# Context attention: the last three head pairs regrouped one group of scores sooner, and the product banks weighed first in the gated part

## The chip, the cores and the metric

One core of a Trainium2 chip runs the whole program. The metric is device time in microseconds, the median of several executions; lower is better. TensorE (PE) multiplies, with its weight loads listed apart as PEld. VectorE (DVE), ScalarE (ACT) and GpSimd (POOL) do the elementwise work. SyncE (SP) computes nothing here: it issues DMA transfers, one after the other.

## The reference

A transformer block over x of shape (2, 1024, 256) with a context of shape (2, 154, 192), in float32, 16 heads of 64:

```python
h = layernorm(x, ln1);  x = attention(h, h,       sa_*) + x
h = layernorm(x, ln2);  x = attention(h, context, ca_*) + x
h = layernorm(x, ln3)
p = h @ ff_w1 + ff_b1
a, gate = p[..., :1024], p[..., 1024:]
out = (a * gelu(gate)) @ ff_w2 + ff_b2 + x
```

Attention is softmax(q kᵀ / 8) v for each head, and then a product with `wo`.

## The kernel before

The program is one long order written out by hand: no scheduler moves anything, and every engine runs its own instructions in the order in which the loops emit them. Self-attention fills the first two thirds of the span, then comes context attention, then the gated part (the feed-forward layer).

**Context attention** works on 16 units, one for each batch and pair of heads (8 pairs for each of 2 batches); below, "pair 13" is unit 13. The scores of a unit are made in three groups of token tiles (3, 3 and 2 tiles of 128), so there are 48 groups, counted by `c`; `CA` is 48 and `len(CG)` is 3. The loop over `c` emits, for each group, the scores (`sc`, L828), then maxima, exponentials and the scaling with the reciprocal sums. Two groups later `cross_drain` transposes the probabilities on VectorE into a ring of three units (`pT_ca`, L872).

**Regrouping.** `cross_regroup(c)` copies one unit's transposed probabilities from the ring into the buffer `pairs`, by eight DMAs of 128 KB issued from SyncE (L889). The buffer has two halves, `a2` = 0 and 1; the first four DMAs fill half 0, the last four half 1. There is one such buffer (a part of the tile `wf`), so a unit's regrouping must wait for the products of the unit before, which read it.

**Products.** `cross_weigh(c)` runs `cross_values` for two parts, `a2` = 0 and then 1. Part `a2` multiplies the values `v_ca` with half `a2` of `pairs` for two of the four quarters of the tokens, into two PSUM banks (`poc`, L908; quarters 0 and 2 in part 0, 1 and 3 in part 1). Part 0 takes its banks from the pool of sums (`sum_tile`, two banks), part 1 from the pool of products (`mm_tile`, two banks). The four banks are then copied into `o_ca` (L922): all on VectorE in context attention, in the gated part half on VectorE and half on ScalarE. One `o_ca` tile holds two pairs (`HP` is 2), and `out_piece` multiplies it with `ca_wo` into `py_ca` (L471), one product for each pair in turn; VectorE adds the result to x (L478).

A unit's last group is `c = 3 ui + 2`, transposed at `3 ui + 4`; its regrouping stands at `3 ui + 5`, its products at `3 ui + 7`. For the last units the count runs on into the gated part, where `c = 48 + k`: unit 14 is weighed at k = 1 and unit 15 at k = 5. `context_values`, once for every two units, makes a new `v_ca`; the six DMAs that complete it (L800, L805) are put on the list `later` and issued at the end of the same step, after `cross_regroup` in that step.

**The gated part** takes two steps for each block of 128 features. `gate_first` makes `pa`, `pb` and `pc` (L1029), where `pa` is in a product bank; `gate_second` adds to them, and ScalarE takes GELU from `pa` (L1066). Then, in each step:

```python
cross_drain(c)
if k % 2:
    cross_weigh(c - 1 if k == len(CG) + 2 else c)
cross_regroup(c)
```

`gate_first` of the next block asks for a product bank again, and so does each `py_ca` of the gated part. The dictionary `pools` is empty before the gated part and holds one entry from its beginning on.

Of the kernel before, what the change touches and what calls it, by code (L numbers as in the profile page):

```python
# [18 lines left out]
def tile_transformer_block(ctx: ExitStack, tc: tile.TileContext, a: dict, out: bass.AP):  # L19
# [11 lines left out]
    HP = NPAIR // NQ  # L31
# [182 lines left out]
    hT, vs, qk, oT = {}, {}, {}, {}  # L214
# [347 lines left out]
    def run(piece):  # L562
        done = piece()
        if done is not None:
            (adds if getattr(done, "adds", False) else stores).append(done)

    def flush(queue):
        for fn in queue:
            fn()
        queue.clear()  # L570
# [160 lines left out]
    CG = [(t, min(TG, NT - t)) for t in range(0, NT, TG)]  # L731
    CA = len(CG) * NU
# [144 lines left out]

    def cross_regroup(c):

        ui, n = divmod(c - len(CG) - 2, len(CG))  # L880
        if n != 0 or not 0 <= ui < NU:
            return
        for a2 in range(2):
            for a4 in range(P // KB):
                half, e = divmod(a4, 2)
                own = slice(a4 * KB, (a4 + 1) * KB)
                src = slice((2 * half + a2) * KB, (2 * half + a2 + 1) * KB)
                blocks = pTc["ring"][src, ui % 3, :2 * NM].rearrange("p (m e) j q -> p m e (j q)", e=2)
                nc.sync.dma_start(  # L889
                    out=pTc["pairs"][own, a2].rearrange("p m j q -> p m (j q)"), in_=blocks[:, :, e])  # L890

    def cross_values(ui, a2):

        b, pr = units[ui]
        v, v0 = vs["ca", b, pr // 2], pr % 2 * P
        if a2 == 0 and pr % HP == 0:
            oT["ca", b, pr // HP] = pt_.tile([P, HP, S], F32, tag="oT", name=f"o_ca{b}_{pr}")  # L900
        quarters = (a2, 2 + a2)
        po = {a4: (mm_tile if a2 else sum_tile)(f"poc_{ui}_{a4}") for a4 in quarters}
        for m in range(NM + 1):
            for a4 in quarters:
                r0 = a4 // 2 * QG
                r = slice(r0, r0 + QG)
                for j in range(2):
                    nc.tensor.matmul(  # L908
                        po[a4][j * DH:(j + 1) * DH, :NT * KB],
                        lhsT=v[r, m + a2 * (m == NM), v0 + j * DH:v0 + (j + 1) * DH],  # L910
                        rhs=pTc["pairs"][r, a2, m, j] if m < NM else
                        pTc["ring"][r, ui % 3, NB - 1, j, :],
                        start=(m == 0), stop=(m == NM),
                        tile_position=(r0, j * DH),
                    )
        dst = oT["ca", b, pr // HP][:, pr % HP, :].rearrange(
            "p (t a q) -> p t a q", a=P // KB, q=KB)

        def store():
            for a4 in quarters:  # L920
                copy = nc.scalar.copy if pools and a4 // 2 else nc.vector.tensor_copy
                copy(dst[:, :, a4, :], po[a4][:, :NT * KB].rearrange("p (t q) -> p t q", q=KB))  # L922

        return store
# [18 lines left out]
    def cross_weigh(c):  # L943

        ui, n = divmod(c - 2 * len(CG) - 1, len(CG))
        if n == 0 and 0 <= ui < NU:
            for part in range(2):
                run(lambda: cross_values(ui, part))
            flush(stores)

# [4 lines left out]
    wsum, wh, ub, psum, pools = {}, {}, {}, {}, {}  # L955
# [156 lines left out]
    with tc.manual_schedule():  # L1112
# [59 lines left out]
        for p in range(SA):  # L1172
# [19 lines left out]
            ui, n = divmod(p, 2 * SH)  # L1192
# [8 lines left out]
            if hg == LAG:  # L1201
# [5 lines left out]
                if n == SH + LAG and ui in (0, 1, NU - 1):  # L1207

                    pr = {0: 2, 1: 4, NU - 1: 6}[ui]
# [3 lines left out]
        for c in range(CA):  # L1213
# [13 lines left out]
            ui, n = divmod(c, len(CG))  # L1227
# [33 lines left out]
            elif c == 4:  # L1261
                run(lambda: self_values(2 * NU - 1, 1))
            elif n == 0 and ui:
                if nxt:
                    run(lambda: cross_queries(*nxt))
                else:
                    run_work(2, 0)
                run_work(0, 1)
            elif n == 1:

                spare["turned"] = True
                run_work(0, 1, sum_tile if outs else None)
                flush(stores)
                run_work(0, 0, n_sum=1)
                if ui % 2 == 0:
                    run(lambda: context_values(*units[ui]))
                run_work(1, 0)
                flush(adds)
                flush(stores)
                cross_weigh(c)  # L1280
            elif n == 2:
                run_work(0, 1, sum_tile if ui == HP + 1 else None)
                if c == SH + 1:
                    run_work(2, 0)
                elif ui == HP:
                    wo["ca"] = const.tile([P, NPAIR, D], F32, tag="wo", name="ca_wo")
                    later[:0] = [lambda i=i: nc.sync.dma_start(
                        out=wo["ca"][:, i, :], in_=w["ca_wo"][i * P:(i + 1) * P, :])
                        for i in range(NPAIR)]
            cross_regroup(c)  # L1290
            for _ in range(min(2, len(later))):
                later.pop(0)()
# [16 lines left out]
        for k in range(2 * FU):  # L1309
            c = CA + k  # L1310
            if k == 0:
                run_work(0, 0, n_sum=2)
            flush(adds)
            (gate_second if k % 2 else gate_first)(k // 2)
            flush(stores)
            flush(lates)
            if k == 2 * len(CG) + 1:
                norm_beside("ff", B - 1)
# [4 lines that stand above are left out]
            if k == len(CG) + 2:  # L1323
                out_pieces("ca", B - 1, NQ - 1, out_order("ca"))
            if k % (2 * NF) == NF and k < 2 * FU - 2 * NF:
                token_sums(k // (2 * NF) + 1)
            for _ in range(min(2, len(sums))):
                run(sum_slot)
            flush(stores)
            run_work(0 if k == 1 else 1 + k % 2, k % 2)  # L1330
            if later and (k <= len(CG) + 2 or k > 2 * NF):
                later.pop(0)()
# [37 lines left out]
```

## Time and profile before

| | |
|---|---|
| median of 3 runs | 1082.71 us (1082.28 to 1084.15) |
| the profiled execution | 1084.96 us, of which the span is 1083.2 us |
| granted TensorE clock | 1.000 over the span |
| 885 to 930 us: busy | PE 43.26, PEld 34.21, DVE 29.79, ACT 19.37, POOL 24.89 us; DMA share 0.36 |
| 930 to 1083 us: busy | PE 149.08, DVE 75.09, ACT 42.72, POOL 68.79 us; DMA share 0.04 |

Times in the profile are microseconds from the span's start. A line of the timeline gives the start, the length, the engine, the line of the kernel, the operation, the tiles (out<-in) and the number of instructions; in brackets stands how long the engine was idle just before, and what released it. SPq is SyncE's queue, and the length of one of its lines is that of issuing, not of the transfer. A releaser is inferred from semaphores: of a wait for several it names the one that came last by the profile. The busy time of TensorE is partly modelled, so a stall shows best in the gaps between weight loads. One float32 product shows as two weight loads and two matmuls.

### The profile page before, as it was taken

The numbers are of one execution on the slowest core, as the hardware profiler recorded it, in microseconds if no ns is written. First come the engines' busy times: TensorE is split into PE (matmuls) and PEld (weight loads), VectorE is DVE, ScalarE is ACT, GpSimd is POOL, SyncE is SP. The second block draws the span as 40 slices with busy tenths as digits, with TensorE's granted clock in tenths as the row PEclk, the third lists the DMA queues.
The fourth block names the chain that finished last, engine by engine and source line by source line (L and its number), as shares of the span: only waits on it lengthen the run. The fifth ranks groups of instructions, "written<-read, shape, count | busy, mean of one in ns | idle before, by whom it ended". The sixth has DMA issues, their size and how long they took to land.

```text
span 1083.2 us, 46388 instructions
## 1 busy us (share of the span) xinstructions
PE 1067.0 (99%) x19156; PEld 703.2 (65%) x19156; DVE 878.7 (81%) x1297; ACT 643.5 (59%) x2062; POOL 727.1 (67%) x1552
## 2 busy tenths in 40 slices
PE   8999999999999999999999999999999999999998
PEld 6556556556565565575665655566776677788887
DVE  5799999998989989999999889968877887654442
ACT  5766666777667657666776776656555554242321
POOL 2677777777777777677777777776756785475321
PEclk9999999999999999999999999999999999999999
DMA  3222122112111121111111101136765545000000
GB/s 91 68 70 52 39 48 53 43 43 50 32 43 34 30 50 38 34 43 34 33 42 25 43 14 38 29 79 150 191 157 125 119 107 118 1 10 15 11 14 30
DMA packets 104724, 60.81 MB, mean 56 GB/s; under 512 B 32378, under 2 KB 95298, under 8 KB 104514
## 3 DMA queue, kind: packets, MB, share of 16 engines
q1 hardware_dynamic: 103138, 57.07, 22.2%
q8 instruction: 151, 2.47, 1.0%
q10 hardware_dynamic: 1376, 0.79, 0.2%
q14 instruction: 59, 0.48, 0.1%
HBM read 27.91 MB, written 2.10 MB: 28 GB/s over the span
## 4 chain that ended last, share of the span: by engine, by line
PE 83%; DVE 4%; POOL 4%; DMA 3%; SPq 2%; ACT 2%; issue 1%; POOLq 0%; DVEq 0%; ACTq 0%
PE po L549 18%; PE s L497 17%; PE py_sa L471 5%; PE pf L1095 5%; PE py_ca L471 5%; PE pk_sa L366 4%; PE pv_sa L397 4%; PE poc L908 4%; PE pq_ca L366 4%; PE pq_sa L366 4%; PE pb L1029 4%; DMA st<-st 3%; PE sc L828 2%; PE pa L1029 2%; PE pc L1029 2%; SPq L518 2%
## 5 line engine op out<-in xcount | busy, mean ns | idle before, releaser
L619 POOL TENSOR_SCALAR p<-p,rd,ee 128x512 f32<-128x512 f32 x512 | 390.4, 768 | 90.8 <-DVE rd L609 87.7
L508 ACT ACTIVATE p<-s,st 128x512 f32<-128x512 f32 x512 | 345.0, 686 | 171.1 <-DVE st L681 163.7
L681 DVE TENSOR_REDUCE st<-s 128x2 f32<-128x1024 f32 x256 | 308.5, 1206 | 56.9 <-issue 19.0
L644 DVE STREAM_TRANSPOSE pT<-p 128x1024 f32<-128x1024 f32 x256 | 302.7, 1219 | 2.4 <-POOL p L619 2.1
L497 PE MATMUL s<-k_sa,q_sa 64*32 64x512 f32 x4096 | 252.8, 591 | 3.3 <-ACT p L508 2.5
L549 PE MATMUL po<-pT,v_sa 64*32 64x256 f32 x8192 | 237.1, 376 | 1.0 <-DVE pT L644 1.0
L549 PEld LDWEIGHTS po<-pT,v_sa 64*32 64x32 f32 x8192 | 172.9, 106 | 76.2 <-issue 31.2
L497 PEld LDWEIGHTS s<-k_sa,q_sa 64*32 64x32 f32 x4096 | 78.4, 106 | 104.6 <-issue 57.6
L845 ACT ACTIVATE p<-sc,neg 128x154 f32<-128x154 f32 x256 | 96.1, 403 | 83.0 <-DVE rden L853 79.3
L856 POOL TENSOR_SCALAR p<-p,rden 128x154 f32<-128x154 f32 x256 | 96.8, 398 | 56.7 <-DVE rden L853 56.5
L508 ACT ACTIVATION_READ_ACCUMULATOR p<-s,st 128x1 f32 x512 | 103.9, 203 | 0.0
L526 POOL TENSOR_TENSOR dd<-st 128x8 f32<-128x8 f32 x128 | 25.6, 200 | 74.9 <-DMA st<-st 73.0
L397 PEld LDWEIGHTS pv_sa<-sa_wv,hT_ln 64*128 64x128 f32 x1024 | 58.5, 188 | 14.2 <-issue 8.4
L397 PE MATMUL pv_sa<-sa_wv,hT_ln 64*128 64x128 f32 x1024 | 61.8, 275 | 0.0
L471 PE MATMUL py_ca<-ca_wo,o_ca 128*128 128x256 f32 x256 | 60.0, 382 | 0.5 <-DVE o_ca L922 0.5
L366 PE MATMUL pq_ca<-hT_ln,ca_wq 64*64 64x512 f32 (+1 forms) x544 | 60.1, 590 | 0.0
L471 PE MATMUL py_sa<-sa_wo,o_sa 128*128 128x256 f32 x256 | 59.7, 385 | 0.2 <-ACT v_sa L406 0.2
L471 PEld LDWEIGHTS py_sa<-sa_wo,o_sa 128*128 128x128 f32 x256 | 47.3, 190 | 18.2 <-issue 6.9
L834 DVE TENSOR_REDUCE neg<-sc 128x6 f32<-128x924 f32 (+1 forms) x48 | 47.9, 998 | 13.7 <-PE sc L828 13.3
L366 PE MATMUL pq_sa<-hT_ln,sa_wq 64*32 64x512 f32 (+1 forms) x976 | 56.6, 586 | 0.0
L366 PE MATMUL pk_sa<-hT_ln,sa_wk 64*32 64x512 f32 x960 | 56.2, 590 | 0.3 <-ACT q_sa L381 0.3
L845 ACT ACTIVATION_READ_ACCUMULATOR p<-sc,neg 128x1 f32 x256 | 56.1, 219 | 0.0
(121 smaller groups left out, 1418.9 us busy)
## 6 DMA issues: line engine op xcount, KB each, us to landing
wf<-pT_ca SPq DMA_DIRECT2D x128, 128.0 KB
st<-st SPq DMA_DIRECT2D x512, 1.0 KB
v_sa<-v_sa SPq DMA_DIRECT2D x32, 256.0 KB
sa_wq<-in_L_xattn_sa_wq_dram SPq DMA_DIRECT2D x32, 128.0 KB
sa_wk<-in_L_xattn_sa_wk_dram SPq DMA_DIRECT2D x32, 128.0 KB
sa_wv<-in_L_xattn_sa_wv_dram SPq DMA_DIRECT2D x32, 128.0 KB
ca_wq<-in_L_xattn_ca_wq_dram SPq DMA_DIRECT2D x32, 128.0 KB
wf<-in_L_xattn_ff_w_dram SPq DMA_DIRECT2D x12, 256.0 KB
```

The source lines that it names most:

```text
L366: nc.tensor.matmul(pq[r][f:f + m, at:at + n], lhsT=wt[own, c, f:f + m], rhs=h[own, c, t0:t0 + n], start=(c == 0), stop=(c == NH - 1), tile ...
L397: nc.tensor.matmul(pv[r][:, i * P:(i + 1) * P], lhsT=h[own, c, i * P:(i + 1) * P], rhs=wt[own, c, :], start=(c == 0), stop=(c == NH - 1), ...
L471: nc.tensor.matmul(py[:, e * D:(e + 1) * D], lhsT=o[:, i, (t + e) * P:(t + e + 1) * P], rhs=wo[kind][:, g * HP + i, :], start=(i == 0), st ...
L497: nc.tensor.matmul(sc[a4 * KB:(a4 + 1) * KB, j, :], lhsT=q[r, c:c + KB], rhs=k[r, h * HB:(h + 1) * HB], start=True, stop=True, tile_positi ...
L508: nc.scalar.activation(pr[:, j, :], sc[:, j, :], AF.Exp, bias=st[:, 0, 0, i, j:j + 1], accum_out=st[:, 0, 1, i, j:j + 1],)
L549: nc.tensor.matmul(po[a2][d:d + KB, :QH // 2], lhsT=v[r, t, e, d:d + KB], rhs=pT[r, d // DH * NK + n, :], start=(t == 0 and e == 0), stop= ...
L619: nc.gpsimd.tensor_scalar(pr[:, j, :], pr[:, j, :], own["rd"][:, c:c + 1], own["ee"][:, 0, c:c + 1], op0=ALU.mult, op1=ALU.mult,)
L644: nc.vector.transpose(halves[h][:, :, c:c + KB], slots[p]["p"][i].rearrange("p j (n k) -> p (j n) k", k=KB))
L681: nc.vector.tensor_reduce(st[:, 0, 0, i, :], sc[i], AX.X, ALU.max, negate=True)
L845: nc.scalar.activation(pr_[:, j, i, :T], sc[:, j, i * T:(i + 1) * T], AF.Exp, bias=neg[:, j, i:i + 1], accum_out=den[:, j, i:i + 1],)
L856: nc.gpsimd.tensor_scalar(pr_[:, j, i, :T], pr_[:, j, i, :T], rden[:, j, i:i + 1], 1.0, op0=ALU.mult, op1=ALU.mult,)
L1029: nc.tensor.matmul(into[:, :BT], lhsT=lhs, rhs=wh[pair][i], start=first, stop=True, skip_group_check=True)
```

## The change

`cross_regroup` subtracts one group less for `c` above 42. Units 13, 14 and 15 are so regrouped at c = 43, 46 and 49 instead of 44, 47 and 50: in the step in which their last transposes are emitted, and in which the unit before them is weighed. For unit 13 this is also the step of the last `v_ca`, whose six DMAs now stand behind the regrouping on SyncE; between the regroupings of units 13, 14 and 15 there is otherwise nothing on SyncE in either kernel, apart from those six.

In `cross_weigh` the two parts run in the order 1, 0 once `pools` is filled, which is for units 14 and 15. The four copies follow in the same order. `cross_values` makes a new `o_ca` tile when there is none yet, instead of in part 0. No instruction is added or removed on any of the engines' lists.

```diff
     def cross_regroup(c):

-        ui, n = divmod(c - len(CG) - 2, len(CG))
+        ui, n = divmod(c - len(CG) - (1 if c > CA - 6 else 2), len(CG))
         if n != 0 or not 0 <= ui < NU:
             return
...
     def cross_values(ui, a2):
...
-        if a2 == 0 and pr % HP == 0:
+        if ("ca", b, pr // HP) not in oT:
             oT["ca", b, pr // HP] = pt_.tile([P, HP, S], F32, tag="oT", name=f"o_ca{b}_{pr}")
...
     def cross_weigh(c):

         ui, n = divmod(c - 2 * len(CG) - 1, len(CG))
         if n == 0 and 0 <= ui < NU:
-            for part in range(2):
+            for part in (1, 0) if pools else (0, 1):
                 run(lambda: cross_values(ui, part))
             flush(stores)
```

## The prediction

> **What bounds the kernel now.** The page comes first: TensorE is busy for 99% of the span and carries most of the chain that ended last, so a change counts only where TensorE stands still or starts something sooner.
>
> ```profile
> PE 1067.0 (99%) x19156; PEld 703.2 (65%) x19156; DVE 878.7 (81%) x1297; ACT 643.5 (59%) x2062; POOL 727.1 (67%) x1552
> PE 83%; DVE 4%; POOL 4%; DMA 3%; SPq 2%; ACT 2%; issue 1%; POOLq 0%; DVEq 0%; ACTq 0%
> ```
>
> Second, the waits of the weight loads (PEld) from 890 to 930 us, the stretch that holds all the edited steps: three long ones, each put down to an o_ca copy.
>
> ```profile
> PEld poc L908 <- DVE o_ca L922: 1.1, 1, 1.1
> PEld py_ca L471 <- DVE o_ca L922: 1.0, 1, 1.0
> PEld pa L1029 <- DVE o_ca L922: 1.0, 1, 1.0
> ```
>
> Third, the timeline of the weight loads around the first of them: the products of head pair 13 (poc), beside the same products of pair 12, which ran freely (first and last two lines below). Columns: start, length, engine, line.
>
> ```profile
> 889.27 0.64 PEld L908 LDWEIGHTS poc<-wf,v_ca 64*64 64x64 f32 x16 [0.33 <-issue]
> 891.70 1.42 PEld L828 LDWEIGHTS sc<-kT,q_ca 64*64 64x64 f32 x40
> ...
> 897.68 0.27 PEld L908 LDWEIGHTS poc<-wf,v_ca 64*64 64x64 f32 x4
> 898.23 0.44 PEld L908 LDWEIGHTS poc<-wf,v_ca 64*64 64x64 f32 x10 [0.28 <-issue]
> 899.46 0.22 PEld L908 LDWEIGHTS poc<-wf,v_ca 64*64 64x64 f32 x4
> 900.83 0.44 PEld L908 LDWEIGHTS poc<-wf,v_ca 64*64 64x64 f32 x10 [1.14 <-DVE o_ca L922]
> 902.82 0.30 PEld L471 LDWEIGHTS py_ca<-ca_wo,o_ca 128*128 128x128 f32 x2 [0.21 <-issue]
> ```
>
> The named releaser is wrong here. Pair 13's second part needs no o_ca copy; it needs the last four transfers of its own regrouping. SyncE's timeline shows those transfers queued behind six loads of v_ca:
>
> ```profile
> 888.48 1.17 SPq L800 DMA_DIRECT2D v_ca<-v_ca  x2
> 889.74 2.48 SPq L805 DMA_DIRECT2D v_ca<-ends  x4
> 892.32 25.34 SPq L889 DMA_DIRECT2D wf<-pT_ca  x24
> ```
>
> By the semaphore events of the trace, pair 13's eight transfers were issued between 892.32 and 898.90; the fourth landed at 898.13, the sixth at 899.36, the eighth at 900.72. The three late starts of poc (898.23, 899.46, 900.83) each follow one of these by 0.1 us. The other two waits are real o_ca waits, in the gated part:
>
> ```profile
> 913.64 0.42 DVE L922 COPY o_ca<-poc 128x256 f32<-128x256 f32 x1 [0.87 <-PE poc L908]
> 914.12 0.30 PEld L1029 LDWEIGHTS pa<-hT_ln,wf 128*128 128x128 f32 x2 [0.97 <-DVE o_ca L922]
> 925.39 0.42 DVE L922 COPY o_ca<-poc 128x256 f32<-128x256 f32 x1 [0.87 <-PE poc L908]
> ```
>
> There `poc_1` sits in the product bank that the next `pa` (914.12) or `py_ca` (925.86) wants, and it is copied out last.
>
> **Part A, pair 13 regrouped one group sooner.** Its eight transfers go ahead of the six v_ca loads on SyncE. They now wait for pair 12's products, which read the same buffer: the reads that release the first transfer end at 890.35, those that release the fifth at 891.64. At about 0.63 us per issue the eight run from 890.4 to 895.5, instead of 892.3 to 898.9.
> One issue in this stretch was held: the fifth lasted 1.89 us (895.04 to 896.93) where the median of L889 is 596 ns, and it began 0.1 us after a 16 KB instruction packet that took 1.62 us (894.93 to 896.55). Thirteen of the 128 issues of this line took over 0.7 us, nearly one per pair, so I leave such a hold in place at 894.9: it then hits the eighth issue, which would land where the fifth did before, at about 898.7. TensorE asks for the fifth to eighth at 897.68 plus half of pair 12's 2.43 us, 898.9. So they are just in time, and if nothing is held they land at about 897.3.
> What that is worth: free running, the products need 2.43 us of weight loads (889.27 to 891.70), the 16 loads of the last scores 16/40 of 1.42 = 0.57, the switch 0.21; py_ca would start at 897.68 + 3.21 = 900.89 instead of 902.82, 1.93 us sooner. But py_ca's second product (third weight load, 903.14 before) reads pair 13's o_ca, and VectorE is full until its first two copies end at 900.71. The other two follow at once (0.80 before, spaced 0.37), end at 901.45, and the third load goes at 901.51. Gain 903.14 - 901.51 = 1.63 us: VectorE is what comes late next.
> Bounds: at best 1.93; if the 1.3 us hold belongs to this one execution alone, the stall it causes is absent from the timed runs as well, the eighth transfer lands there at 899.4 anyway, and the gain is about 0.5. If the hold delays more than one of the moved transfers, about 1.0 is left. I take 1.6, since a hold of this kind comes with nearly every pair.
> [...]
> The six v_ca loads now issue from about 896.9 to 900.8 and land by about 903; pair 14, the first to read them, starts at 910.79 (909.2 after the gain). Cost nothing under a cover of 6 us. [...]
>
> **Part A, pairs 14 and 15.** Before the change nothing stands on SyncE between these regroupings and the one ahead, and both begin only when VectorE's transposes end (900.11 and 912.17 in the trace). Issuing them earlier in the program moves nothing: 0. Pair 14 can start up to 0.7 us later, when SyncE is through with v_ca (900.8); its last landing goes from 907.1 to 907.8, still 1.4 us ahead of its use.
>
> **Part B, product banks first.** Same instructions, other order; units 14 and 15 only. At pair 14, `poc_1` is copied at the 912.35 place and its bank is free long before `pa` asks. `pa` loads at 913.15 (last poc load ends) + 0.21 switch = 913.36, not 914.12: 0.76 us. At pair 15 the next work is py_ca, which reads all four copies in its second product; only its first, two loads of 0.216 us, can go ahead: 0.43 us. What could come late instead: the new first part needs the bank that GELU releases (ACT ends at 910.50, needed from 910.79) and the regrouping's transfers five to eight first. Pair 15's last landed at 919.45; its start is now tied to pair 14's later-read half and gains only about 0.3 us, so 919.1, against a need at 922.53 - 1.63 - 0.76 = 920.1. One microsecond of cover: cost 0 here, up to 0.5 if a hold falls there.
>
> **Sum.** 1.63 + 0.76 + 0.43 = 2.8 us. Behind 926 us, TensorE's remaining waits (about 3 us, on VectorE and GpSimd) hang on work that itself follows TensorE, so the shift reaches the end. The profiled execution took 1084.96 us (span 1083.2) and would take 1082.2; it lies 2.25 above the median of the runs, where the same difference gives 1082.71 - 2.8 = 1079.9.
>
> **Rivals.** *Smaller, within 0.2%* (2.17 us, about what a measurement of this kernel can tell from no change): the hold was an accident, part A is 0.5 to 1.0, the sum 1.7 to 2.1, time 1080.6 to 1081.0. For it: fed by one execution; against: thirteen long issues in one trace.
> *Part B alone works*: pair 13 is bounded by VectorE anyway. VectorE has no gap from 893.5 to 900.7, but then 1.31 us idle before the 902.03 copy; so it is not the bound through the stall. Gain 1.2, time 1081.5, same side as the first rival.
> *Slower*: SyncE falls behind. After pair 13 it issues 14 transfers where 8 stood before pair 14's use. If two more holds of 1.3 us fall on them and on pair 14's own eight, the last lands at 907.8 + 2.6 = 910.4, 1.2 us after it is needed (909.2), which eats under half; it decides from a landing after about 912 (the gain is gone) and passes 0.2% slower from one after about 914.2, with a time of 1085. Against it: 1.4 us of cover and a DMA share of 36% in this stretch.
>
> **How the numbers follow.** Forecast 0.64, the two smaller cases together 0.28, slower 0.08 (part of it within 0.2%: 0.02). The forecast's own bounds are 0.3 us up (1.93 for part A) and 0.6 down; the smaller cases reach 1081.5, and the runs before spread by 0.4 below and 1.4 above their median. Range 1079.0 to 1081.9.
>
> **What the next profile would show.** Right: pair 13's eight issues ahead of v_ca's six on SyncE; no load gap over 0.2 us inside pair 13's poc; a gap of about 0.3 us after py_ca's first product there; the gap before `pa` at pair 14 down from 0.97 to 0.2; py_ca at pair 15 split after its first product. Wrong: pair 13's poc still waits for a landing, or pairs 14 or 15 wait for theirs.

## The result, and the profile after

The changed kernel took 1081.62 us (median of 16 runs, 1080.70 to 1082.21); the kernel before, in 16 runs of the same comparison, 1083.45 (1082.10 to 1085.08). The ratio is 0.9982, 95% interval [0.9975, 0.9989]: 1.8 us less by the medians. Forecast were 1079.9 and 2.8 us less. The time lies inside the range, near its upper end. 1.8 us is less than the 2.17 us that the prediction named as what can be told from no change; it had given that case 0.30.

The profiled execution has a span of 1079.9 us (1083.2 before). The page, the same two rows as before:

```profile
PE 1065.9 (99%) x19156; PEld 696.7 (65%) x19156; DVE 878.4 (81%) x1297; ACT 644.4 (60%) x2062; POOL 727.2 (67%) x1552
PE 85%; POOL 4%; DMA 4%; DVE 3%; SPq 2%; issue 1%; ACT 1%; POOLq 0%; DVEq 0%; ACTq 0%
```

TensorE still carries most of the chain, and every engine has as many instructions as before. The waits of the weight loads from 890 to 930 us (line, releaser, us in total, times, longest): all three long ones, 1.1, 1.0 and 1.0 us, are gone.

```profile
PEld py_ca L471 <- issue: 0.8, 3, 0.4
PEld pa L1029 <- issue: 0.4, 1, 0.4
PEld py_ca L471 <- ACT o_ca L922: 0.3, 1, 0.3
```

The timeline of the weight loads of pair 13: both parts now run through, with no gap over 0.1 us inside `poc`, and `py_ca` follows with all 16 loads.

```profile
897.15 0.71 PEld L908 LDWEIGHTS poc<-wf,v_ca 64*64 64x64 f32 x16
897.93 0.37 PEld L908 LDWEIGHTS poc<-pT_ca,v_ca 64*64 64x64 f32 x8
898.36 0.80 PEld L908 LDWEIGHTS poc<-wf,v_ca 64*64 64x64 f32 x16
899.23 0.37 PEld L908 LDWEIGHTS poc<-pT_ca,v_ca 64*64 64x64 f32 x8
899.66 0.63 PEld L828 LDWEIGHTS sc<-kT,q_ca 64*64 64x64 f32 x16
900.50 3.32 PEld L471 LDWEIGHTS py_ca<-ca_wo,o_ca 128*128 128x128 f32 x16 [0.22 <-issue]
```

SyncE's timeline shows the exchange of places: pair 13's eight, then v_ca's six, then pairs 14 and 15.

```profile
889.86 5.92 SPq L889 DMA_DIRECT2D wf<-pT_ca  x8
895.87 1.18 SPq L800 DMA_DIRECT2D v_ca<-v_ca  x2
897.15 2.49 SPq L805 DMA_DIRECT2D v_ca<-ends  x4
899.75 16.26 SPq L889 DMA_DIRECT2D wf<-pT_ca  x16
```

By its single issues the hold stayed where it was: the first seven took 0.58 to 0.60 us each, the eighth 1.31 (894.46 to 895.78), beside a 16 KB instruction packet at 894.46. The eighth transfer landed at 897.61. The loads that read it begin at 898.36: 0.75 us of cover.

In the gated part, in the same timeline of weight loads, the gap before `pa` fell from 0.97 to 0.39 us (0.2 was forecast), and the one gap of 0.97 before pair 15's `py_ca` became 0.39 and 0.35, split after the first product:

```profile
911.22 0.30 PEld L1029 LDWEIGHTS pa<-hT_ln,wf 128*128 128x128 f32 x2 [0.39 <-issue]
...
922.38 0.30 PEld L471 LDWEIGHTS py_ca<-ca_wo,o_ca 128*128 128x128 f32 x2 [0.39 <-issue]
923.02 2.89 PEld L471 LDWEIGHTS py_ca<-ca_wo,o_ca 128*128 128x128 f32 x14 [0.35 <-ACT o_ca L922]
```

**One stretch for all kernels.** Where pair 13's products begin differs from execution to execution by up to 2 us without any edit ahead of them (897.15 to 899.21 us among the profiles of kernels that are the same up to there). So the profiles are compared below by the stretch from pair 13's first weight load of `poc` to the end of the span (differences are taken before rounding). It is 185.48 us before and 182.75 after: 2.73 us less. Of these, 1.78 are gone when pair 14's products end, 0.58 go at `pa`, 0.37 at pair 15's `py_ca`. The rest, from the next `pa` on, is 153.96 against 153.97 us: all but 0.01 is kept. The spans differ by 3.3 us because this execution also reached pair 13 0.53 us sooner.

### The profile page after: what moved, and what is told of

It reads as the page before. It is cut to its first block, busy times and chain, and to the rows that moved or that the text cites. A ratio compares the mean times of both kernels' runs of the same rounds, so it can differ in the third digit from the quotient of the medians.

```text
span 1079.9 us, 46388 instructions
## 1 busy us (share of the span) xinstructions
PE 1065.9 (99%) x19156; PEld 696.7 (65%) x19156; DVE 878.4 (81%) x1297; ACT 644.4 (60%) x2062; POOL 727.2 (67%) x1552
## 4 chain that ended last, share of the span: by engine, by line
PE 85%; POOL 4%; DMA 4%; DVE 3%; SPq 2%; issue 1%; ACT 1%; POOLq 0%; DVEq 0%; ACTq 0%
PE po L549 19%; PE s L497 18%; PE py_sa L471 5%; PE pf L1095 5%; PE py_ca L471 5%; PE pv_sa L397 5%; PE pk_sa L366 4%; PE pq_ca L366 4%; PE pq_sa L366 4%; PE poc L908 4%; PE pb L1029 4%; PE sc L828 3%; PE pa L1029 2%; PE pc L1029 2%; DMA st<-st 2%; SPq L518 2%
## 5 line engine op out<-in xcount | busy, mean ns | idle before, releaser
L497 PE MATMUL s<-k_sa,q_sa 64*32 64x512 f32 x4096 | 250.2, 591 | 2.9 <-ACT p L508 2.2
L549 PEld LDWEIGHTS po<-pT,v_sa 64*32 64x32 f32 x8192 | 169.6, 106 | 78.5 <-issue 31.3
```

The lines of the kernel that those rows point to most:

```text
L497: nc.tensor.matmul(sc[a4 * KB:(a4 + 1) * KB, j, :], lhsT=q[r, c:c + KB], rhs=k[r, h * HB:(h + 1) * HB], start=True, stop=True, tile_positi ...
L549: nc.tensor.matmul(po[a2][d:d + KB, :QH // 2], lhsT=v[r, t, e, d:d + KB], rhs=pT[r, d // DH * NK + n, :], start=(t == 0 and e == 0), stop= ...
```

## Experiments

My theory: pair 13's stall is its own transfers, late because six loads of `v_ca` and one held issue stand ahead of them on SyncE; the hold belongs to a place in TensorE's program; the two parts of the change add. Rivals: VectorE bounds pair 13 (part B alone works); the hold is an accident of one execution (part A is worth 0.5); SyncE falls behind. Ratios are against the kernel before, with their 95% intervals.

**Part A alone.** The changed `cross_regroup` (and the `o_ca` tile made on first use), the parts in the old order.

> Only the earlier regrouping, the product parts in the old order. My theory (pair 13's transfers were queued behind six v_ca loads; the hold at the instruction packet stays but strikes a transfer that is early enough): no load gap over 0.2 us inside pair 13's poc, the gaps of 0.97 us before pa at pair 14 and before py_ca at pair 15 both stay, time 1.2 to 1.8 us below the kernel before (0.9983 to 0.9989). Rival (the stall at pair 13 was an accident of one execution): time at most 0.5 us below. Rival (all is in the bank order): no change.

Ratio 0.9988 [0.9977, 0.9998], 1083.33 us against 1084.82. The stall in `poc` is gone, the two gated waits remain; weight-load waits, 890 to 930 us:

```profile
PEld pa L1029 <- DVE o_ca L922: 1.0, 1, 1.0
PEld py_ca L471 <- DVE o_ca L922: 1.0, 1, 1.0
```

The stretch is 183.70 us: 1.78 less than before. VectorE's work did not change, so it did not bound pair 13: the rival "part B alone works" falls.

**Part B alone.** The changed order in `cross_weigh`, the old `cross_regroup`.

> Only the order of the product parts, regrouping at the old place. My theory: pair 13's stall is there again in this profile (poc starts three times late, last start right after the eighth landing), the two gaps of 0.97 us shrink to about 0.4 and 0.4 + 0.35, time 0.8 to 1.2 us below the kernel before (0.9989 to 0.9993). Rival (the stall was an accident): this profile shows pair 13's poc running through, and the time is 1.8 us below.

Ratio 0.9996 [0.9986, 1.0007]: the timed runs can tell no difference (0.4 us less by the medians, where 0.8 to 1.2 was forecast). In the profile the gated waits shrink as in the changed kernel and pair 13's stall is back:

```profile
PEld poc L908 <- DVE o_ca L922: 1.2, 1, 1.2
PEld py_ca L471 <- issue: 0.8, 3, 0.4
...
PEld pa L1029 <- issue: 0.4, 1, 0.4
PEld py_ca L471 <- ACT o_ca L922: 0.3, 1, 0.3
```

The stretch is 184.43 us, 1.06 less than before. Of that 0.12 is a shorter hold (1.77 us on pair 13's fifth issue, where it was 1.89), which leaves 0.94 for the order itself; between part A alone and the whole change lie 183.70 - 182.75 = 0.95. The parts add.

**Only the loads of v_ca later.** The kernel before, with the six transfers of the last `v_ca` put behind pair 13's regrouping, which stays at its old place.

```diff
+    held_loads = []
...
-            later.insert(0, lambda: [
+            own = held_loads if b == B - 1 and pr == NPAIR - 2 else later
+            own.insert(0, lambda: [
...
-            later.insert(1, lambda: [
+            own.insert(1, lambda: [
...
+            if c == CA - 4:
+                later[:0] = held_loads
```

> The kernel before, with nothing moved but the six v_ca loads of pairs 14 and 15, which are issued behind pair 13's regrouping instead of ahead of it; the regrouping keeps its place in the program. If it is the order on SyncE's queue that counts, this gives what the earlier regrouping gives alone: pair 13's eight issues begin as soon as pair 12's products let them (about 890), no stall in pair 13's poc, 1.2 to 1.8 us below the kernel before. If it is the earlier place in the program that counts, no change.

Ratio 0.9987 [0.9977, 0.9996], and a stretch of 183.71 us, that of part A alone (183.70) to 0.01. So what part A buys is the exchange of places on SyncE, and the earlier regrouping as such is one way to get it.

**All units sooner.** The changed kernel with units 1 to 15 regrouped one group sooner.

```diff
-        ui, n = divmod(c - len(CG) - (1 if c > CA - 6 else 2), len(CG))
+        ui, n = divmod(c - len(CG) - (1 if c > 2 * len(CG) - 1 else 2), len(CG))
```

> The changed kernel, with pairs 1 to 15 all regrouped one group sooner instead of only the last three. My theory: the other pairs have other TensorE work between scores and products that covers their landing, so nothing is gained there; within 0.7 us of the changed kernel, that is 0.9976 to 0.9990 of the kernel before. Rival: every odd pair stalls behind its six v_ca loads as pair 13 did, and each gives up to 1 us more, 0.992 to 0.996. Rival: v_ca and weight loads that now wait behind the regroupings come late, slower than the changed kernel by over 1 us.

I expected next to nothing, and was wrong: ratio 1.0058 [1.0042, 1.0075], 1091.63 us against 1084.82. The stretch from pair 13 on is 182.75 us, exactly that of the changed kernel; all of the loss comes before. TensorE's own waits from 710 to 935 us begin with two that the kernel before does not have:

```profile
PE pq_ca L366 <- DMA ca_wq<-in_L_xattn_ca_wq_dram: 4.6, 3, 2.7
PE pv_ca L788 <- DMA ca_wv<-in_L_xattn_ca_wv_dram: 1.7, 2, 1.5
```

In the earlier units SyncE has weight loads queued (`ca_wq`, `ca_wv`). An early regrouping stands on SyncE until the unit before has been multiplied, and the weights behind it land late: from 710 to 935 us SyncE's waits of L889 for `poc` come to 41.1 us, against 9.4 in the kernel before. This is the mechanism of the prediction's slower rival, in a place where the changed kernel does not go: for its three units only six loads stand behind a wait, and they have their cover. The two waits sum to 6.3 us of the 9.0 by which this kernel reaches pair 13 later than the changed one (906.15 against 897.15); a third new one, of 1.1 us before `pv_ca`, is put down to ScalarE, and what makes up the rest was not followed.

**Where the hold sits.** The kernel before, with more of the idle transposes that TensorE does at the start (the two texts call them warm-up), one profiled execution each. That moves every later step of TensorE against the 16 KB instruction packets, which come about every 255 recorded TensorE instructions (weight loads and products; the median of each profile is 251 to 256, single counts lie far to both sides), and leaves SyncE's list as it is. First 64 more:

```diff
-        for _ in range(27):
+        for _ in range(27 + 64):
```

> The kernel before, with 64 more of its idle warm-up transposes at the start (91 instead of 27): 128 more TensorE instructions (a weight load and a multiply each) ahead of everything, nothing else changed. The whole program starts some 10 us later, so only the stretch of pair 13 is read, in times relative to its own steps. In the runs so far a 16 KB instruction packet comes about every 256 TensorE instructions, so the packet that stood at 894.9 stands half a block, 128 instructions, sooner: 4 us before, beside the v_ca loads of L805. Theory (the hold belongs to the place of TensorE's own instruction fetch): no issue of L889 of pair 13 takes over 0.7 us, one issue of L800 or L805 does, by 0.9 to 1.9 us; as it stands ahead of pair 13's eight in the same queue, the eighth landing is as late as before and pair 13's poc stays at 4.4 to 4.8 us with its stall. Rival (the hold is an accident or belongs to the regrouping's own transfers): the long issue is again the fourth to sixth of L889, or there is none and poc is shorter by over 1 us.

Then 112 more:

> The kernel before, with 112 more warm-up transposes at the start (139 instead of 27): 224 more TensorE instructions, so the 16 KB instruction packets stand 224 sooner, which is 32 later than one block sooner: counted in the profile of before, at the places of 887.4 (ahead of the v_ca loads) and 897.2 (at or behind the eighth issue of pair 13, if none before it is held). Only the stretch of pair 13 is read, relative to its own steps. Theory (the hold goes where the packet goes): the first seven issues of pair 13 all take under 0.7 us, its landings five to seven come about 1.2 us sooner relative to the first poc load than in the kernel before, the stall inside poc shrinks and poc falls from 4.7 to between 3.0 and 4.2 us (the upper end if the eighth issue is held). Rival (an accident, or a property of the regrouping's transfers): a hold of over 1 us again among the first seven issues, poc 4.4 us or more.

The lengths of `poc` in these two texts count from a semaphore wait that stands 0.63 us ahead of the first weight load. In that count 64 more gave 4.26 us, 112 more 4.58 us, the kernel before 4.72. SyncE's timeline, first of 64 more, then of 112 more, then of the kernel before in a second profile (told of below):

```profile
895.08 3.31 SPq L805 DMA_DIRECT2D v_ca<-ends  x4
898.50 5.26 SPq L889 DMA_DIRECT2D wf<-pT_ca  x8
```

```profile
901.66 2.48 SPq L805 DMA_DIRECT2D v_ca<-ends  x4
904.24 6.49 SPq L889 DMA_DIRECT2D wf<-pT_ca  x8
```

```profile
889.31 2.48 SPq L805 DMA_DIRECT2D v_ca<-ends  x4
891.89 6.63 SPq L889 DMA_DIRECT2D wf<-pT_ca  x8
```

With 64 more, four L805 issues take 3.31 us instead of 2.48 and pair 13's eight only 5.26 instead of 6.63: the hold (1.41 us, 896.35 to 897.76, packet at 896.44) has moved to the third L805 issue, as the theory said. It is shorter than forecast (0.8 us over the usual issue, where 0.9 to 1.9 was expected), and `poc` with 4.26 us lies under the 4.4 to 4.8 that the theory gave. With 112 more it is on the seventh of pair 13 (1.74 us from 908.35, packet at 908.34), where I had counted on the eighth or behind it; so `poc` did not fall to 4.2 us: a hold of over 1 us among the first seven and 4.4 us or more is, to the letter, what the rival had said. The packet came 0.8 us sooner, against the products, than my count put it. What speaks against the rival is the place: in all three the held issue is the one that starts within 0.1 us of the packet, and which one that is moves with TensorE's instruction count, once off the regrouping altogether. So neither "accident" nor "property of the regrouping's transfers" stands. An 8 KB instruction packet of another queue also starts beside the held issue of the kernel before (895.07); with 64 and 112 more it starts beside other issues of pair 13 (900.54 and 906.99), and these take 0.60 and 0.65 us. So around pair 13 it is the 16 KB packet that counts; further on in the kernel before, an issue of 0.85 us (913.52) starts just behind an 8 KB packet alone (913.46).

The landings show a second effect, which I had not counted with. In the traces each transfer of L889 has sixteen landing events. For the two transfers issued last ahead of the packet, without any hold, the sixteenth event comes 1.2 to 1.7 us after the fifteenth: in the kernel before for the third and fourth (896.61 and 897.78, 896.90 and 898.12), with 112 more for the fifth and sixth (909.33 and 910.99, 910.08 and 911.32). The first late start of `poc` follows the last of these events by 0.1 us, at 898.23 and at 911.42. So beside the packet a part of transfers already issued comes late too, and this is why landings five and six did not come sooner with 112 more.

The price follows the hold. Over part A alone (183.70 us) the stretch is longer by 1.82 us with a hold of 1.95, by 1.78 with 1.89, by 1.66 with 1.74 and by 1.32 with 1.41. Less what the hold adds to the usual issue of 0.59 us, each leaves 0.46 to 0.51 us: the part of the stall that would be there without any hold, which the prediction had put at 0.5.

**Only pair 13 sooner, with the new order.**

```diff
-        ui, n = divmod(c - len(CG) - (1 if c > CA - 6 else 2), len(CG))
+        ui, n = divmod(c - len(CG) - (1 if c in (CA - 5, CA - 4) else 2), len(CG))
```

> The change with only unit 13 regrouped one group sooner; units 14 and 15 are regrouped at the old places, and the order of the parts is the changed one. Theory (for units 14 and 15 nothing else stands on SyncE, so their earlier place moves nothing): within 0.3 us of the changed kernel, ratio to before about 0.998; the issue times of pair 14's eight are unchanged against the changed kernel within 0.3 us. Rival (pair 15's earlier place matters now that part 1 comes first): slower than the changed kernel by 0.3 to 1 us, with a wait of pair 15's poc for its own landings.

Ratio 0.9980 [0.9971, 0.9989], stretch 182.77 us against 182.75: the earlier regrouping of pairs 14 and 15 is worth nothing, as forecast.

**The output products of pair 15 later.**

```diff
-            run_work(0 if k == 1 else 1 + k % 2, k % 2)
+            run_work(0 if k in (1, 5) else 1 + k % 2, k % 2)
```

> The changed kernel with one edit more: in step k = 5 the output products py_ca of the last pairs are not emitted behind pair 15's products at once, but one step later, so that the next block's pa comes first and fills TensorE's wait for the four o_ca copies (in the profile after: gaps of 0.39 and 0.35 us before and inside py_ca at 922.4). Theory (these gaps are only a wait for the copies): both gaps fall to the switch of 0.2 us or less, about 0.4 to 0.6 us faster than the changed kernel, ratio to before about 0.9978. Rival (the product banks are then held longer and the wait returns at a later pa or py_ca): within 0.2 us of the changed kernel.

Ratio 0.9977 [0.9966, 0.9988], beside 0.9980 of the changed kernel on the same chip. The stretch is 182.56 us, 0.2 less than the changed kernel's, where 0.4 to 0.6 was forecast. In size that is the rival's number, but not for its reason: no wait comes back later. The gap of 0.35 us for the copies is gone, but not the gap ahead of it:

```profile
922.92 0.30 PEld L1029 LDWEIGHTS pa<-hT_ln,wf 128*128 128x128 f32 x2 [0.39 <-issue]
```

This `pa` does not read the copies and still waits 0.39 us. So the 0.39 us after `poc` come without any wait for the copies, and are not, as I had it, 0.2 and a rest of that wait. This kernel is the best of those run, by an amount that only the profile can tell.

**The timing against itself.** The changed kernel gained 2.73 us in the profiles and less in the timed runs, so I ran it again beside the two kernels above, and once more beside the kernel before timed against itself.

> The changed kernel itself again, beside the two others on the same chip, so that they can be compared with it. Theory (holds of about 1.3 us in a usual run, so that pair 13's part is worth about 1.3 and the order 0.4 to 0.8): 1.7 to 2.1 us faster than before, ratio 0.9980 to 0.9985. Rival (the profile's 2.7 us is the usual gain): ratio 0.9975 or less.

> The kernel before, timed against itself, to see how far two sets of runs of one kernel lie apart here, and for a second profile of its stall. Both theories: ratio 1.000 within 0.001. Theory (the stall of pair 13 is in every run, as long as the hold beside it): the second profile shows 31.7 to 32.2 us from the first poc load of pair 13 to the pa that follows pair 15 (32.15 in the first profile, 29.41 in the changed kernel), with a hold of 1.3 to 1.9 us on one of the issues ahead of pair 13's eighth landing. Rival (the first profile's stall was unusually long): under 31.5 us.

> The changed kernel once more, beside the kernel before timed against itself. Theory (the gain of the timed runs is the profile's, 2.3 to 2.7 us, and the first comparison was low by chance): ratio 0.9976 to 0.9979. Rival (timed runs hold less than the profiled ones): 0.9980 to 0.9984 again, with the kernel before against itself at 1.000.

| run | ratio [95%] | medians, us | stretch, us |
|---|---|---|---|
| changed kernel, first comparison | 0.9982 [0.9975, 0.9989] | 1081.62 / 1083.45 | 182.75 |
| changed kernel, second | 0.9980 [0.9970, 0.9989] | 1082.44 / 1084.80 | 182.76 |
| changed kernel, third | 0.9980 [0.9971, 0.9988] | 1082.85 / 1084.76 | 182.77 |
| kernel before against itself | 1.0008 [0.9999, 1.0017] | 1085.60 / 1084.76 | 185.52 |

The profiles repeat to 0.04 us: 185.48 and 185.52 before, 182.75 to 182.77 after, with the hold of the kernel before on the same fifth issue again (1.89 and 1.95 us). The timed runs give 1.8 to 2.4 us less, and the same kernel against itself came out 0.84 us apart. In the third comparison the changed kernel is 1.9 us under one set of runs of the kernel before and 2.75 under the other. Both times 0.9980 fell at the edge of the band of the text that expected less in the timed runs than in the profile. Yet 2.73 us would be a ratio of 0.9975, at the edge of the first interval and inside the other two. The second profile of the kernel before has its hold, and 32.18 us from the semaphore wait of pair 13's `poc` to the `pa` that follows pair 15 (31.7 to 32.2 forecast).

## Why the prediction was right or wrong

- **The mechanism of part A** was right: the releaser named in the profile was wrong, the transfers were late, the exchange on SyncE ended it, and the hold stayed beside its packet at 894.5 and met the eighth issue, just in time (forecast to land at 898.7, landed at 897.61; pair 13 began 0.53 sooner, so that is 0.56 us better than forecast). What it left out is that a part of the transfers issued just ahead of the packet also lands late (the sixteenth event 1.2 to 1.7 us after the fifteenth in the old order, 0.65 and 0.75 us here for the sixth and seventh); the moved ones had cover for that too (the last event of the sixth came at 896.66, of the seventh at 897.03, ahead of the loads at 898.36).
- **Its size**: 1.63 forecast, 1.78 measured. The term that was off is the VectorE wait after `py_ca`'s first product (0.3 forecast), which cost TensorE nothing. VectorE's timeline has the four copies in one piece:

```profile
899.47 1.38 DVE L922 COPY o_ca<-poc 128x256 f32<-128x256 f32 x4
```

They end at 900.85, and `py_ca`'s third load starts at 900.90, 0.40 us after its first (900.50) where the kernel before has 0.32. So the load did wait, by 0.08 us, but the matmuls did not: the third starts 0.54 us after the first in both profiles. I had the time from the first load of `poc` to that of `py_ca` 0.14 us too short (3.21 instead of 3.35) and the end of the copies 0.07 too late.
- **Part B**: 0.76 + 0.43 forecast, 0.58 + 0.37 measured. At pair 14 what failed is the switch from `poc` to the next product, taken as 0.21 us from a switch of another kind (`sc` to `py_ca`); it is 0.39. At pair 15 the last copy ends 0.92 us after `poc`'s last load in both profiles, and `py_ca`'s second product starts 0.45 us sooner, as forecast; 0.08 of this goes again just behind the wait, where the next matmul follows after 0.29 us instead of 0.22.
- **Sum in the profile**: 2.82 forecast, 2.73 measured; the terms that were too small and too large nearly cancel. Two slips in the recorded sums change nothing: the smaller case adds up to 1.7 to 2.2 us, not 2.1, and the "about 3 us" of waits behind 926 us contain the 1.0 us ahead of pair 15's `py_ca`.
- **What it says of the time** is less sure. By the time alone, 1081.62 lies above the 1080.6 to 1081.0 of the smaller rival and beside the 1081.5 of "part B alone works"; it is the profiles that decide against both. The forecast of 1079.9 went from 1082.71, the median of three runs; over 16 runs the kernel before took 1083.45, and that is 0.74 of the 1.72 us by which 1079.9 was too low. The other 1.0 is the step "the same difference" in the sum: 2.8 us of the profile against 1.8 in the timed runs. The comparisons together do not settle whether the timed runs have a shorter hold or whether their scatter makes 2.73 look like 1.8 to 2.4; the same kernel against itself is 0.84 apart, and the hold can be seen only in a profile. This stays open.
- **The rivals.** The accident: not so; all five profiles of the old order (the kernel before twice, part B alone, the two with more transposes at the start) have a hold of 1.4 us or more beside the packet, ahead of pair 13's eighth landing. By the prediction's estimate an accident would have made part A about 0.5 us; the stretch says 1.78 and lets 1.3 of it rise and fall with the held issue. By what means an instruction packet and a held issue on SyncE go together no run here shows. SyncE falling behind: not in this change (pair 15's last landing at 917.78 for loads at 919.63); it did when all units were regrouped sooner (41.1 us of SyncE's waits of L889 for `poc` against 9.4), with a ratio of 1.0058.
- **Pairs 14 and 15 sooner: 0** was right (182.77 against 182.75).

## What to carry to other kernels

A releaser in the profile is a guess for a wait on several semaphores (here a `poc` load was put down to an `o_ca` copy and waited for transfers, the last of which landed at 900.72, 0.11 us ahead of its start): when the named engine had nothing to do with it, look at the queue of the transfers that feed the waiting instruction, and at what stands ahead of them there. A waiting transfer moved forward on SyncE held up what was queued behind it: for three units that cost nothing, with fifteen pair 13 was reached 9.0 us later, 6.3 of them in waits for weights, so read each place by itself. When the gain sought is below the scatter of whole runs, measure in the profile from the first edited step to the end of the span, over several profiles, and time the kernel before against itself to learn what the timing can tell.

## What the runs showed that I had not expected

- Around pair 13, the issue on SyncE that starts within about 0.1 us of a 16 KB instruction packet takes 1.3 to 1.95 us instead of 0.6 (1.89 and 1.95 in the kernel before, 1.31 in the changed kernel, 1.77 in part B alone, 1.41 and 1.74 with 64 and 112 more transposes), and which one it is can be moved by adding TensorE instructions hundreds of microseconds earlier (from the fifth transfer of pair 13 to a load of `v_ca`, or to the seventh). Elsewhere it is not as exact: in the kernel before the issue at 877.20, 0.09 us ahead of its packet, took 0.65 us, and the next one, 0.6 us behind the packet's start, 1.15.
- The switch of TensorE from `poc` (64x64 tiles) to a 128x128 product leaves 0.39 us between weight loads, also where the operands had long been ready; from `sc` (also 64x64) to `py_ca` it leaves 0.22. The products ahead of the switch differ too (256 columns and 376 ns a matmul in `poc`, 154 and 291 ns in `sc`), so the gap may be the end of the last matmul; no run here separates this from the change of tile shape.
- From pair 13 to the end, the profiled executions of one kernel repeat to 0.04 us (185.48 and 185.52 before, 182.75 to 182.77 after); what scatters by 2 us (pair 13 begins at 897.15 to 899.21) lies before.
